# A second level of the seven-product scheme, over four batches at a time, in a graph network's aggregation

## The chip, the cores and the metric

The kernel runs on one core of one Trainium2 chip. All times are microseconds of device time of that core. Each is the median of the runs of one kernel, and every ratio is against runs of the kernel before on the same chip in the same rounds. Experiments sent at different times fell on two chips, on which the kernel before took 2066.7 and 2067.3, so differences between experiments of one or two us mean nothing. All runs told here were in the fast state.

## The reference, cut to what matters

Sixteen batches of 1024 nodes with 128 features pass through one plain graph layer (layer 0) and a gated layer of five steps (the GRU). Every step multiplies the same 1024 x 1024 adjacency matrix with the state of every batch; this product is called the aggregation.

```python
# layer 0
x = layernorm(x + (einsum('nm,bmo->bno', adj, x @ weight) + bias))
# layer 1, five times; in_matrix and out_matrix are both adj
m_in  = einsum('nm,bmd->bnd', in_matrix, h)
m_out = einsum('nm,bmd->bnd', out_matrix, h)          # the same product
av = concatenate([m_in, m_out], -1)
u3 = h @ u3_w.T + u3_b
z  = sigmoid(av @ w3_w.T + w3_b + u3)
r  = sigmoid(av @ w4_w.T + w4_b + u3)                 # u3 is common to z and r
hv = tanh(av @ w5_w.T + w5_b + (r * h @ u5_w.T + u5_b))
h  = (1 - z) * h + z * hv
# after the steps
x = layernorm(x + h)
```

All is fp32. There are six aggregations of sixteen batches (one in layer 0, five in the GRU).

## The kernel before

It already uses the seven-product scheme (seven block products in place of eight, paid for with sums of blocks) on one level. The adjacency is cut into 2 x 2 blocks, and a pair of batches makes the two block columns of the other factor. Each of the seven products is four matmuls of 512 columns (each of them two instructions in the trace). DVE (the vector engine) makes the four operand sums and adds the products up; the last batches' update lies under the next pair's first product.

```python
def sums(q, s):                      # operand sums of a pair: DVE, in SBUF
    nc.vector.tensor_sub(t[:, 0], block(q, 0, 1), block(q, 0, 0))
    nc.vector.tensor_sub(t[:, 1], block(q, 1, 1), t[:, 0])
    nc.vector.tensor_sub(t[:, 2], block(q, 1, 1), block(q, 0, 1))
    nc.vector.tensor_sub(t[:, 3], block(q, 1, 0), t[:, 1])

def product(n, pm, start):           # 4 matmuls, 512 columns each
    for c in range(CH):
        nc.tensor.matmul(pm, right[n][:, c, :], left[n][:, c, :],
                         start=(start and c == 0), stop=(c == CH - 1))

# [...] in aggregate: the chain of seven products and the adds out of PSUM
pa = bank("a"); product(1, pa, True);  nc.scalar.copy(p1, pa)
pb = bank("b"); product(6, pb, True);  nc.vector.tensor_add(u2, pb, p1)
product(2, pa, False);                 nc.scalar.copy(out_of[0, 0], pa)
product(7, pb, False);                 nc.vector.tensor_add(u3, pb, p1)
pc = bank("c"); product(5, pc, True);  nc.vector.tensor_add(out_of[1, 1], pc, u3)
product(4, pb, False);                 nc.vector.tensor_add(out_of[1, 0], pb, p1)
product(3, pc, False);                 nc.vector.tensor_add(out_of[0, 1], pc, u2)

# [...] in gates: u3 is copied to SBUF, and DVE adds it to both gates
nc.scalar.copy(u3[h], pu)
for w_t, b_t, dst in ((w4_t, br, rh_t[b]), (w3_t, bz, z_t[b])):   # [...] for each half of the columns
    nc.tensor.matmul(pg, w_t, m_t[b][:, cols], start=True, stop=True)
    nc.vector.tensor_add(dst[:, cols], pg, u3[h])
    nc.scalar.activation(dst[:, cols], dst[:, cols], AF.Sigmoid, bias=b_t)
```

The sixteen batches go in four groups of two pairs, each group through layer 0 and then its five steps.

## Time and profile before

| | before |
|---|---|
| median of the first three runs, lowest to highest | 2067.68, 2064.82 to 2069.21 us |
| profiled span, mean granted TensorE clock | 2062.0 us, 0.991 |
| TensorE (PE) busy | 96% |
| DVE / ScalarE (ACT) / GpSimd (POOL) busy | 53% / 27% / 7% |
| one GRU step of a pair, all of it TensorE busy | 43.19 us, so 86.4 us for four batches |

The page's first lines tell how long each engine was busy, the next ones the same in 40 slices of the span, in tenths; "PEclk" there is the share of its clock that TensorE was granted. The chain is what ended last, followed back from wait to wait. A line of a timeline has its start, its duration, the engine, the source line, the operation with what it writes and reads, the shapes, and how many instructions were taken together; at its end, in brackets, stands how long the engine had been idle and what it waited for. The lines that carry the reading are in the prediction below. They say that TensorE's own instruction stream is the time, and that DVE and POOL have room.

### The profile page before, as it was taken

How to read it: one execution, taken by the hardware profiler on the slowest of the kernel's cores; microseconds unless marked ns; L12 is line 12 of the kernel's file. 1: busy time of each engine (PE TensorE's matmuls, PEld its weight loads, DVE VectorE, ACT ScalarE, POOL GpSimd, SP SyncE). 2: the span in 40 equal slices, each digit the busy share in tenths (PEclk: the TensorE clock that was granted, in tenths of full speed). 3: DMA queues.
4: the chain of work that ended last, by engine and by line, in shares of the span. 5: the costliest groups of instructions: out<-in, count | busy, mean ns of one | idle time of the engine just before them, and what ended most of it. 6: DMA issues, size and time to landing. Idle time of an engine off the chain costs nothing.

```text
span 2062.0 us, 14771 instructions
## 1 busy us (share of the span) xinstructions
PE 1988.8 (96%) x5381; PEld 929.3 (45%) x5381; DVE 1100.5 (53%) x2284; ACT 563.0 (27%) x906; POOL 147.8 (7%) x190
## 2 busy tenths in 40 slices
PE   6999999999999999999989999999998999999994
PEld 4544444444444444444444444444444444444442
DVE  4544555446764554445675454455566544555447
ACT  1022333223103332233202322233220222333221
POOL 4200000001220000000231000000022000000001
PEclk9999999999999999999999999999999999999997
DMA  4000000000000000000000000000000000000000
GB/s 135 0 1 0 0 0 0 21 0 21 21 21 0 0 0 1 0 21 21 0 31 10 1 0 0 1 21 0 21 21 21 0 0 0 0 1 0 0 0 41
DMA packets 7561, 22.57 MB, mean 11 GB/s; under 512 B 1472, under 2 KB 2368, under 8 KB 7488
## 3 DMA queue, kind: packets, MB, share of 16 engines
q1 hardware_dynamic: 3168, 10.62, 1.5%
q0 software_dynamic: 2304, 8.39, 1.0%
q10 hardware_dynamic: 2016, 2.62, 0.4%
q8 instruction: 42, 0.69, 0.1%
q14 instruction: 31, 0.25, 0.0%
HBM read 13.24 MB, written 8.39 MB: 10 GB/s over the span
## 4 chain that ended last, share of the span: by engine, by line
PE 87%; DVE 9%; POOL 2%; DMA 1%; issue 1%; ACT 0%; POOLq 0%; ACTq 0%; SPq 0%; DVEq 0%
PE pb L199 20%; PE pc L199 13%; PE pg L275 13%; PE pa L199 13%; PE pu L268 6%; PE ph L287 6%; PE ph L286 6%; PE pt L307 3%; POOL rstd L162 2%; DVE stats L158 2%; DVE y L164 1%; DVE res L164 1%; DVE y L309 1%; DVE mv L159 1%; PE po L242 1%
## 5 line engine op out<-in xcount | busy, mean ns | idle before, releaser
L275 PE MATMUL pg<-m,w_t 128*128 128x512 f32 x640 | 291.9, 599 | 0.2
L270 ACT COPY u<-pu 128x512 f32<-128x512 f32 x160 | 92.2, 577 | 572.7 <-PE pu L268 572.7
L199 PE MATMUL pa<-a,rows 128*128 128x512 f32 x512 | 230.2, 592 | 0.0
L199 PE MATMUL pb<-a,t 128*128 128x512 f32 x512 | 230.2, 592 | 0.0
L275 PEld LDWEIGHTS pg<-m,w_t 128*128 128x128 f32 x640 | 118.3, 190 | 162.4 <-issue 124.4
L276 DVE TENSOR_TENSOR rh<-pg,u 128x512 f32<-128x512 f32 x160 | 110.7, 692 | 144.8 <-PE pg L275 144.8
L236 POOL TENSOR_TENSOR x<-x,b_bc 128x128 f32<-128x128 f32 x128 | 70.9, 566 | 1362.0 <-ACT hv L289 381.7
L286 PE MATMUL ph<-m,w_t 128*128 128x512 f32 x320 | 163.5, 592 | 0.0
L287 PE MATMUL ph<-rh,u_t 128*128 128x512 f32 x320 | 163.4, 592 | 0.0
L289 ACT ACTIVATE hv<-ph,bh 128x512 f32<-128x512 f32 x160 | 110.0, 687 | 176.2 <-PE ph L287 130.1
L290 DVE TENSOR_TENSOR hv<-hv,h 128x512 f32<-128x512 f32 x160 | 111.0, 694 | 83.4 <-ACT hv L289 83.4
L199 PEld LDWEIGHTS pb<-a,t 128*128 128x128 f32 x512 | 97.3, 190 | 122.5 <-issue 122.5
L268 PE MATMUL pu<-h,u_t 128*128 128x512 f32 x320 | 150.5, 592 | 0.0
L220 DVE TENSOR_TENSOR u3s<-pb,p 128x512 f32<-128x512 f32 x40 | 27.6, 691 | 217.9 <-PE pb L199 217.9
L199 PEld LDWEIGHTS pa<-a,rows 128*128 128x128 f32 x512 | 94.8, 190 | 107.1 <-issue 107.1
L277 ACT ACTIVATE rh<-rh,br 128x512 f32<-128x512 f32 x160 | 115.4, 722 | 85.7 <-DVE rh L276 80.5
L277 ACT ACTIVATE z<-z,bz 128x512 f32<-128x512 f32 x160 | 115.9, 724 | 41.5 <-DVE z L276 41.3
L199 PE MATMUL pc<-s,rows 128*128 128x512 f32 x256 | 115.1, 592 | 0.0
L199 PE MATMUL pc<-s,t 128*128 128x512 f32 x256 | 115.1, 592 | 0.0
L199 PE MATMUL pb<-s,t 128*128 128x512 f32 x256 | 115.1, 592 | 0.0
L291 DVE TENSOR_TENSOR hv<-hv,z 128x512 f32<-128x512 f32 x160 | 111.3, 696 | 3.7
L292 DVE TENSOR_TENSOR h<-h,hv 128x512 f32<-128x512 f32 x160 | 111.1, 694 | 3.9
(344 smaller groups left out, 2144.5 us busy)
## 6 DMA issues: line engine op xcount, KB each, us to landing
x<-in_x_dram SPq DMA_DIRECT2D x16, 512.0 KB, 4.4
out_dram<-y POOLq DMA_DIRECT2D x16, 512.0 KB, 3.0
adj<-in_adj_dram SPq DMA_DIRECT2D x4, 512.0 KB, 4.2
adj<-in_adj_dram ACTq DMA_DIRECT2D x4, 512.0 KB, 5.3
w_rows<-in_L_gnn_w_w_dram ACTq DMA_DIRECT2D x3, 128.0 KB, 3.9
u_rows<-in_L_gnn_u_w_dram ACTq DMA_DIRECT2D x2, 64.0 KB, 1.8
w_sb<-in_L_gnn_weight_dram SPq DMA_DIRECT2D x1, 64.0 KB, 6.9
b_bc<-in_L_gnn_bias_dram SPq DMA_DIRECT2D x1, 64.0 KB, 6.6
```

The costliest lines, as they stand in the source:

```text
L199: nc.tensor.matmul(pm, right[n][:, c, :], left[n][:, c, :], start=(start and c == 0), stop=(c == CH - 1), skip_group_check=True,)
L268: nc.tensor.matmul(pu, u3_t, h_t[b][:, cols], start=True, stop=True)
L270: nc.scalar.copy(u3[h], pu)
L275: nc.tensor.matmul(pg, w_t, m_t[b][:, cols], start=True, stop=True)
L276: nc.vector.tensor_add(dst[:, cols], pg, u3[h])
L277: nc.scalar.activation(dst[:, cols], dst[:, cols], AF.Sigmoid, bias=b_t)
L286: nc.tensor.matmul(pg, w5_t, m_t[b][:, cols], start=True, stop=False)
L287: nc.tensor.matmul(pg, u5_t, rh_t[b][:, cols], start=False, stop=True)
L289: nc.scalar.activation(hv, pg, AF.Tanh, bias=bh)
L290: nc.vector.tensor_sub(hv, hv, h_t[b][:, cols])
L291: nc.vector.tensor_mul(hv, hv, z_t[b][:, cols])
L292: nc.vector.tensor_add(h_t[b][:, cols], h_t[b][:, cols], hv)
```

## The change

The intent is to cut that stream. The scheme is applied twice: each of the seven block products over 512 x 512 blocks becomes seven products over 256 x 256 blocks, so 49 products stand for 64 where 56 stood. So that a block column of the inner level is still a whole batch of 128 features, four batches (a "quad") are taken together, and two outer products share one chain of seven inner ones: (1, 2) in the first chain, (3) alone in the single chain, then (6, 7) and (5, 4). Two further changes come with it. Layer 0 is done for all batches before the GRU, its result going to DRAM and back. And u3, the common term of the gates, is copied from PSUM into a second PSUM bank, so that both gates' matmuls add onto it and DVE's adds disappear (e1, which keeps this, returns the correct result).

```diff
+    def inner_sums(xs, dst, eng):                       # four sums
+        eng.tensor_sub(dst[0], xs(0, 1), xs(0, 0))
+        eng.tensor_sub(dst[1], xs(1, 1), dst[0])
+        eng.tensor_sub(dst[2], xs(1, 1), xs(0, 1))
+        eng.tensor_sub(dst[3], xs(1, 0), dst[1])
[...]
+    def outer_sums(src):                                # four sums of 1024 columns
+        nc.vector.tensor_sub(tsum[:, 0], hi[:, :, :CH], lo[:, :, :CH])
[...]
     def product(a, pm, start):
-        for c in range(CH):
-            nc.tensor.matmul(pm, right[n][:, c, :], left[n][:, c, :], ...)
+        for o, n in enumerate(ns):
+            for c in range(2):
+                nc.tensor.matmul(pm[:, ts(o, QT)], right[a][:, o, c, :], left[n][a][:, c, :], ...)
+        for hook in hooks.get(a, ()):
+            hook()                  # work of the batches before, between two products
[...]
+    def aggregate(tag, src, hooks):
+        chain(f"12_{tag}", src, (1, 2), into(first), hooks)
+        sums_of(src, (6, 7), nc.vector)
+        nc.vector.tensor_add(c11, two(first[:, 0]), two(first[:, 1]))
+        chain(f"3_{tag}", src, (3,), ..., hooks.get("late", {}))
+        sums_of(src, (5, 4), nc.gpsimd)
+        chain(f"67_{tag}", src, (6, 7), into(room[:, 0:2]), {})
+        nc.vector.tensor_add(p6, p6, first[:, 0])
+        nc.vector.tensor_add(p7, p7, p6)
+        nc.vector.tensor_add(c12, c12, two(p6))
+        chain(f"54_{tag}", src, (5, 4), into(room[:, 2:4]), {})
+        nc.vector.tensor_add(c21, two(p7), two(p4))
+        nc.vector.tensor_add(c22, two(p7), two(p5))
+        nc.vector.tensor_add(c12, c12, two(p5))
[...]  layernorm: the normalising itself moves from DVE to ScalarE
-            nc.vector.tensor_scalar(dst[:, c, :], y[:, c, :], mv[:, c, 0:1], rstd[:, c:c+1], ...)
+            nc.scalar.activation(y[:, c, :], y[:, c, :], AF.Identity, bias=shift[...], scale=rstd[...])
[...]  gates
-            nc.scalar.copy(u3[h], pu)
+            nc.scalar.copy(pz, pu)                       # PSUM to PSUM
+            nc.tensor.matmul(pu, w_t["w4"], agg[:, k, cols], start=False, stop=True, ...)
+            nc.scalar.activation(rh[:, cols], pu, AF.Sigmoid, bias=br)
+            nc.tensor.matmul(pz, w_t["w3"], agg[:, k, cols], start=False, stop=True, ...)
+            nc.scalar.activation(z[:, cols], pz, AF.Sigmoid, bias=bz)
-                nc.vector.tensor_add(dst[:, cols], pg, u3[h])
[...]  layer 0 of quad q, with the projections of quad q-1 between the products of its first chain
+        hooks = {6: [projection(0)], 2: [projection(1)], 7: [projection(2)], 5: [projection(3)]}
+        aggregate(f"x{q}", room, hooks)
[...]  a GRU step
+                def rest(tag=tag):
+                    back_to_rows(tag, 3)
+                    sums_of(rows, (3,), nc.gpsimd)
+                    outer_sums(rows)
+                hooks = {6: [lambda: back_to_rows(tag, 2)], 5: [rest]}
+            aggregate(tag, rows, hooks)
[...]
+            if not last:
+                sums_of(rows, (1, 2), nc.gpsimd)
+            update(tag, 3)
```

In the traces of the changed kernel L260 is the matmul of a product; L222 to L225 are the four inner sums and L243 to L246 the four outer ones; L281, L285, L288, L290 and L292 are the adds of a chain in order; L310 is the first combining add (c11), which stands once in each aggregation and marks the steps; L397 to L399 are the update of the hidden state; L206 and L207 are the statistics of the layer normalisation.

Two passages are cut out of the prediction, where it is marked: what they told of the hardware was not read from a trace or a run of this case. No term of its sum is cut: 91 + 3 x 58 + 8 + 20 x 85.4 + 26 + 22 is the 2029 that stands there, and the 0.215 us of a 256-column instruction is an estimate from the measured 0.429 (512 columns) and 0.11 (128). The lines after the first cut are POOL's and DVE's in the kernel before, while they prepare the adjacency's operands. That a POOL sum "delays DVE by its whole length" is the author's estimate from these lines, in which DVE's add takes 1.56 us for 0.69, so 0.87 more; 0.42 (DVE) and 0.73 (POOL) for 256 columns are estimates too, and the changed kernel's trace has 0.43 and 0.73 for them. That the clock granted to TensorE drops when DVE is late is shown by no line that the prediction quotes; in the changed kernel it was 0.50 after a wait of 4.92 us for a DVE add (below).

> **What bounds the kernel now.** I read the page's busy line and slices first, then the chain of work that ended last, then the groups of instructions with shapes kept apart, then stretches of the timeline.
>
> ```profile
> PE 1988.8 (96%) x5381; PEld 929.3 (45%) x5381; DVE 1100.5 (53%) x2284; ACT 563.0 (27%) x906; POOL 147.8 (7%) x190
> ...
> PE   6999999999999999999989999999998999999994
> ...
> PE 87%; DVE 9%; POOL 2%; DMA 1%; issue 1%; ACT 0%; POOLq 0%; ACTq 0%; SPq 0%; DVEq 0%
> ```
>
> TensorE is busy from end to end and carries 87% of the chain: the time is its instruction stream. Weight loads (PEld) run beside it; DVE has half the span free, POOL nearly all. The timeline of TensorE in one aggregation and in one projection gives the unit costs:
>
> ```profile
> 1002.19 3.60 PE L199 MATMUL pb<-a,t 128*128 128x512 f32 x8
> 1005.62 3.60 PE L199 MATMUL pc<-s,rows 128*128 128x512 f32 x8
> ...
> 55.94 1.95 PE L242 MATMUL po<-w_sb,m_-1_275 128*128 128x128 f32 x16
> 57.72 1.95 PE L242 MATMUL po<-w_sb,m_-1_276 128*128 128x128 f32 x16
> ```
>
> Each fp32 matmul of the program is two instructions. Eight with 512 columns start 3.43 us before the next eight: 0.429 us each, 0.84 ns a column. Sixteen with 128 columns take 1.78 us, 0.11 us each. So the price goes with the columns, and halving the columns must not cost a weight-load penalty: a 256-column instruction should take 0.215 us (an estimate). One GRU step of a pair is 43.19 us (the same gate group stands at 1670.51 and 1713.70 in the chain) and TensorE is busy for all 43.19 of them in the busy times of that stretch. The four groups repeat every 500.3 us (the first layer-0 projection of each group starts at 554.0, 1054.3, 1554.3), so a group is 10 x 43.19 = 432 plus 68 for its two layer-0 pairs.
>
> [...]
>
> ```profile
> 32.16 0.45 POOL L236 TENSOR_TENSOR x<-x,b_bc 128x128 f32<-128x128 f32 x1
> 32.57 1.72 POOL L104 TENSOR_TENSOR s<-a,s 128x512 f32<-128x512 f32 x1
> ...
> 36.80 1.27 POOL L104 TENSOR_TENSOR s<-a,s 128x512 f32<-128x512 f32 x1
> ...
> 32.48 0.69 DVE L102 TENSOR_TENSOR s<-a,a 128x512 f32<-128x512 f32 x1 [0.37 <-ACT a L99]
> 33.09 0.28 DVE L138 COPY w_t<-pt_w 128x128 f32<-128x128 f32 x1
> 33.29 1.56 DVE L103 TENSOR_TENSOR s<-s,a 128x512 f32<-128x512 f32 x1
> ```
>
> Alone a 512-column POOL add takes 1.27 us and a DVE one 0.69. The POOL add at 32.57 first waited for DVE's (1.72), then DVE's at 33.29 stood until POOL's was over (1.56). The two engines take turns, a whole instruction at a time. [...]
>
> **The change part by part.** Counts are per GRU step of four batches ("quad step"), of which there are 20, against 40 pair steps; a quad step of before is 2 x 43.19 = 86.4 us.
>
> *Removed on TensorE.* Aggregation was 2 x 28 matmuls of 512 columns, 112 instructions x 0.429 = 48.0 us. It becomes 49 x 2 matmuls of 256 columns, 196 x 0.215 = 42.2 us: 5.8 us less, an eighth. Gates stay at 80 x 0.429 = 34.3, transposes at 32 x 0.107 = 3.4. TensorE's floor: 79.9 us. Over 20 steps and 4 layer-0 quads the removal is 24 x 5.8 = 139 us, which would be the whole gain if nothing waited.
>
> *DVE.* Removed: the gate adds (L276), 16 x 0.69 = 11 us. Added: chains add 15 x 0.69 + 5 x 0.42 = 12.5 where 20 x 0.69 = 13.8 stood; seven combining adds of 1024 columns at an estimated 1.2 us (0.69 at 512 and 0.34 at 128 give 0.91 ns a column), 8.5; outer operand sums 4 x 1.2 = 4.9 and inner ones 4 x 0.69 = 2.8, for 8 x 0.69 = 5.5 before. Update and reset multiply remain 22.2. Sum 51 us of 80, against 53 of 86: not a bound by itself.
>
> *POOL*, idle in the steps before, gets eight sums of 512 columns (1.27) and four of 256 (about 0.73): 13 us. DVE's operations with two SBUF inputs are 38 us of its 51. By the turn-taking above each POOL sum that meets them delays DVE by its whole length.
>
> *ACT.* The common-term copy goes PSUM to PSUM instead of PSUM to SBUF, same number. Some 31 us a quad step: free.
>
> *What comes onto the path.* A product of the doubled scheme lasts 1.72 us (chain of two) or 0.86 (chain of one), where it lasted 3.43, and DVE's add must be done before the second product after it starts. I walked one steady step by hand in the engines' listed order with the durations above, t = 0 at the last gate matmul. (a) POOL's first sums start at -2.1, between DVE's updates, take turns with them, and the second operand is there at 3.7; TensorE wants it at 1.72: wait 2. (b) DVE, delayed so, ends its updates at 8.4; the first chain add is done at 9.1, TensorE waited since 8.1: 1. (c) The last batch's rows come at 14.4; now DVE has 4.9 of outer sums, POOL the single chain's sums, in turns; POOL's operand is there at 19.9, wanted at 17.8: 2. (d) That chain's first add stands behind inner sums and a combining add until about 26.5: 1. (e) The combining adds behind chain 67: 0.3. (f) Gates: bank rotation and copies, 0.5. Sum about 7 us; the step would be 87, nothing gained. Turn-taking at every meeting is the harshest reading; with half of it the waits are about 4. I take 5.5: 85.4 us a step.
>
> *Layer 0.* Per quad TensorE has 42.2 + 64 x 0.107 = 49. DVE has 31 of sums plus four projections of about 3.9 (two adds, eight statistics at 0.26 a piece, the small ones) = 47, and POOL's bias adds, sums and powers (29 us) hold it up a little. Normalising moves to ACT. I put a quad at 58 where before had 68 a group. The trip through DRAM (16 x 0.5 MB each way) is off the path: the loads of before took 4.4 us each and are issued long ahead.
>
> *Sum.* First layer-0 aggregation done at about 91 us (before had its second pair projected at 92; more operand preparation, no projection yet); 3 x 58 = 174; last projection partly exposed 8; 20 x 85.4 = 1708; first step of each group has transposes of the hidden state and unfinished normalising, 4 x 6.5 = 26; tail 22. Total 2029.
>
> **The rivals.** *TensorE stays the bound*: the waits vanish into its queue. For it: DVE is under two thirds busy; the schedule hoists other products over the waits. Against it: products are half as long and the order is fixed. It would give 2029 - 20 x 4.5 - 4 x 5 = about 1920. *The sums become the bound*: POOL and DVE in full turn-taking plus latencies that I left out, 88 to 90 us a step: 2080 to 2120. For it: walk (a) to (d). *Layer 0 through DRAM stalls the start*: x is loaded twice and saved rows come back; at 4.4 us a transfer against 49 us quads it should hide; if not, 10 to 30 us more. *Seeding costs*: the w4 matmul waits for the ACT copy of the same bank (0.58 us); in the listed order another matmul stands between, so below 0.5 us a batch.
>
> **Range and chances.** Waits of 2 to 9 us a step span 20 x 7 = 140 us, and layer 0 some 30 more; eight in ten lie in 1950 to 2095. Two per cent below 2067.7 is 2026, very near my centre, and waits must be about 5 or less for it. I give 0.46 to faster, 0.46 to the same, and 0.08 to slower, for which waits above 9 are needed. I predict 2028 us.
>
> **What would show it right or wrong.** In the profile after: 256-column instructions at 0.215 us apart (at 0.25 or more the saving is gone and my unit price is wrong). The quad step near 85 us with TensorE busy for about 80. Idle before TensorE put down to POOL and DVE sums (L222, L223, L243 to L246), at the second product of the first and single chains. POOL sums of 512 columns at 1.3 alone and up to 2 beside DVE; DVE's 1024-column sums up to 2.5 in these stretches. No DMA among the large releasers. What would make me wrong: contention smaller than the few early meetings suggest (then near 1920 to 1980), or DVE falling behind for whole stretches, so that the clock granted to TensorE drops as well (then above 2095).

## The result, and the profile after

| | before | after |
|---|---|---|
| median of four runs, lowest to highest | 2068.14, 2064.82 to 2069.21 | 2099.10, 2096.83 to 2100.06 |
| profiled span, clock | 2062.0, 0.991 | 2098.3, 0.976 |
| four batches' GRU step | 86.4 | 86.8 |

The ratio is 1.015, with a 95% interval of 1.013 to 1.017: slower by 1.5%. (Ratios here are the mean time of one kernel's fast runs over that of the other's of the same rounds, so not quite the ratio of the medians quoted.) That is inside the 2% that I called the same, but 70 us above the predicted time and just above the range. An eighth of the aggregation's TensorE work went, and no time with it.

The page's busy line, two rows of its slices and its chain, of the changed kernel:

```profile
PE 1913.4 (91%) x7401; PEld 1311.2 (62%) x7401; DVE 1385.9 (66%) x2191; ACT 710.6 (34%) x1258; POOL 511.9 (24%) x435
...
PE   5987888999999989999999999999999899999995
...
PEclk7999999999999999999999999999999999999997
...
PE 55%; DVE 23%; issue 3%; ACT 2%; POOL 2%; POOLq 0%; DVEq 0%; ACTq 0%
```

TensorE's busy time fell by 75 us (1988.8 to 1913.4), but its share of the chain fell from 87% to 55%, and DVE's rose from 9% to 23%. The bound has become a hand-over between TensorE and DVE. DVE is busy 285 us more than before, although its instructions got fewer (2284 to 2191) and by my sum the step had lost DVE work. That sum was wrong: it put 20 adds of products into four batches' step of before, and the code above has five a pair, so ten. The trace of before has 21.4 us of DVE in a pair's step, so 42.8, where I had 53. Without POOL's sums the changed step has 49.1 (e2 below), and with them 56.0: DVE's own work grew by 6 us a step, and POOL stretched it by 7. The slices 3 to 7, which are layer 0, are the weakest.

Two stretches of the busy times (start:end, length, then busy time and instructions of PE, PEld, DVE, ACT, POOL, then clock and DMA), one quad of layer 0 from one L310 to the next, and one steady step:

```profile
130.01:195.97 65.96, 54.69 (x263) 45.68 (x262) 47.55 (x120) 16.58 (x41) 28.52 (x44) 0.95 0.28 95
...
452.60:539.40 86.80, 82.50 (x310) 54.83 (x309) 56.01 (x67) 29.40 (x48) 18.75 (x12) 1.00 0.00 0
```

My sum had 51 us of DVE and 13 of POOL work in a step; the trace has 56.0 and 18.8. Each has 5 to 6 us more than I had counted, at full clock and with no DMA. In layer 0 a quad takes 66 us, not 58, with TensorE at a mean clock of 0.95 and idle for 11 us.

Now the place where a step begins. The timeline of TensorE, changed kernel:

```profile
400.84 1.89 PE L260 MATMUL pa<-a,rows 128*128 128x256 f32 x8
402.96 1.99 PE L260 MATMUL pb<-e,inner 128*128 128x256 f32 x8 [0.23 <-POOL inner L223]
...
405.66 1.89 PE L260 MATMUL pa<-a,rows 128*128 128x256 f32 x8
408.68 1.99 PE L260 MATMUL pb<-e,inner 128*128 128x256 f32 x8 [1.13 <-DVE first L281]
...
413.12 1.89 PE L260 MATMUL pb<-a,inner 128*128 128x256 f32 x8
414.84 1.89 PE L260 MATMUL pc<-e,rows 128*128 128x256 f32 x8
416.57 1.03 PE L260 MATMUL pa<-s,rows 128*128 128x256 f32 x4
418.80 1.10 PE L260 MATMUL pb<-e,inner 128*128 128x256 f32 x4 [1.21 <-DVE first L290]
...
424.08 0.70 PE L260 MATMUL pa<-s,tsum 128*128 128x256 f32 x2
426.46 1.13 PE L260 MATMUL pb<-s,inner 128*128 128x256 f32 x4 [1.69 <-DVE agg L281]
```

The two lines at 413.12 and 414.84 are 1.72 us apart, eight instructions each: 0.215 us, the price that I had taken. At full speed the instructions before a wait last 1.72 (eight), 0.86 (four) or 0.43 (two), so the second product of a chain could have begun at 402.56, 407.38, 417.43 and 424.51. It began 0.4, 1.3, 1.4 and 1.95 us later: 5.0 us a step. The four places are the (a), (b), (c) and (d) of my walk.

Whom they wait for shows in the timeline of DVE in the same stretch, changed kernel:

```profile
397.68 0.68 DVE L397 TENSOR_TENSOR hvs<-hvs,hid 128x512 f32<-128x512 f32 x1
398.40 1.70 DVE L398 TENSOR_TENSOR hvs<-hvs,tsum 128x512 f32<-128x512 f32 x1
400.20 1.57 DVE L399 TENSOR_TENSOR hid<-hid,hvs 128x512 f32<-128x512 f32 x1
401.70 1.75 DVE L397 TENSOR_TENSOR hvs<-hvs,hid 128x512 f32<-128x512 f32 x1
403.49 1.64 DVE L398 TENSOR_TENSOR hvs<-hvs,tsum 128x512 f32<-128x512 f32 x1
405.21 0.69 DVE L399 TENSOR_TENSOR hid<-hid,hvs 128x512 f32<-128x512 f32 x1
...
417.98 0.68 DVE L290 TENSOR_TENSOR first<-pb,first 128x512 f32<-128x512 f32 x1
...
422.12 2.29 DVE L310 TENSOR_TENSOR agg<-first 128x1024 f32<-128x1024 f32 x1
```

And that of POOL:

```profile
398.29 1.26 POOL L222 TENSOR_TENSOR inner<-rows 128x512 f32<-128x512 f32 x1 [57.98 <-ACT rows L411]
399.51 1.71 POOL L224 TENSOR_TENSOR inner<-rows 128x512 f32<-128x512 f32 x1
401.19 1.71 POOL L223 TENSOR_TENSOR inner<-rows,inner 128x512 f32<-128x512 f32 x1
402.98 1.59 POOL L225 TENSOR_TENSOR inner<-rows,inner 128x512 f32<-128x512 f32 x1
```

The update's three operations take 0.69 us each until POOL's first sum starts at 398.29. From then on, as long as POOL has sums in these lines, each DVE operation, all with two SBUF inputs, takes 1.57 to 1.75 us, and each POOL sum after the first 1.59 to 1.71: they alternate, one whole instruction of the one, then one of the other. When POOL is done (404.57) DVE is back at 0.69. L290 at 417.98, which has one input in PSUM, takes its 0.68 us while a POOL sum is running (L223, 416.94 to 418.64). L310, 1.22 us alone, takes 2.29, and it takes 2.28 or 2.29 in 16 of the 20 steps, all but the first of each group. At the third place (418.80) two sums end together: DVE's L290 at 418.66, which the profile names, and POOL's own L223 at 418.64, so POOL's lateness alone would have made that wait as long.

In layer 0 the same line of adds is late for another reason. TensorE's timeline in the third quad has one line for it:

```profile
184.57 3.78 PE L260 MATMUL pb_x<-a,inner 128*128 128x256 f32 x8 [4.92 <-DVE first L285]
```

and DVE's has what stood ahead of L285 in its queue:

```profile
181.89 0.41 DVE L212 SCALAR_TENSOR_TENSOR shift<-mv,rstd 128x8 f32<-128x8 f32 x1 [2.46 <-POOL rstd L210]
...
183.60 0.26 DVE L206 BATCH_NORM_STATS2 stats<-hid 128x6 f32<-128x128 f32 x1
183.86 0.65 DVE L285 TENSOR_TENSOR first<-pb_x,first 128x512 f32<-128x512 f32 x1
```

The projections of the quad before are hooked in between the products of the first chain, and each brings its normalisation with it. DVE waits 2.46 us for POOL's power, then goes through a batch's statistics, and only then makes the add that TensorE waits for. After those 4.92 us of idling the eight instructions take 3.78 us; 1.89 is normal. The clock granted from 184.5 to 188.4 is 0.50. So this wait costs twice, once as idle time and once as slow products. Shorter waits in layer 0 were followed by slow matmuls too: after 2.48 and 2.68 us (at 111.91 and 309.69) eight instructions of 128 columns took 2.08 and 2.07 us, where 1.05 is normal, at a granted clock of 0.50; after waits of 2.05 us they took 1.16 once and 1.45 once.

### The profile page after: what moved, and what is told of

Read it like the earlier page. It is cut to its first block, busy times and chain, and to the rows that moved or that the text cites. A ratio compares the mean times of both kernels' runs of the same rounds, so it can differ in the third digit from the quotient of the medians.

```text
span 2098.3 us, 20190 instructions
## 1 busy us (share of the span) xinstructions
PE 1913.4 (91%) x7401; PEld 1311.2 (62%) x7401; DVE 1385.9 (66%) x2191; ACT 710.6 (34%) x1258; POOL 511.9 (24%) x435
## 4 chain that ended last, share of the span: by engine, by line
PE 55%; DVE 23%; issue 3%; ACT 2%; POOL 2%; POOLq 0%; DVEq 0%; ACTq 0%
PE pb L260 14%; PE pc L260 9%; PE pu L377 7%; PE seeded L382 6%; PE pu L373 6%; PE pa L260 5%; DVE hvs L398 4%; PE ph L393 4%; PE ph L394 4%; DVE hvs L397 3%; DVE hid L399 3%; POOL rstd L210 2%; DVE tsum L244 1%; DVE inner L225 1%; DVE tsum L245 1%
## 5 line engine op out<-in xcount | busy, mean ns | idle before, releaser
L222 POOL TENSOR_TENSOR inner<-rows 128x256 f32<-128x256 f32 (+1 forms) x38 | 47.4, 1248 | 1077.8 <-ACT rows L411 1021.6
L260 PE MATMUL pb<-e,inner 128*128 128x256 f32 x720 | 179.3, 389 | 48.1 <-DVE first L281 25.1
L397 DVE TENSOR_TENSOR hvs<-hvs,hid 128x512 f32<-128x512 f32 x160 | 127.6, 799 | 90.7 <-ACT hvs L396 90.6
L260 PEld LDWEIGHTS pb<-e,inner 128*128 128x128 f32 x720 | 133.4, 191 | 85.5 <-POOL inner L223 35.4
L377 PE MATMUL pu<-agg,w_t 128*128 128x512 f32 x320 | 169.6, 612 | 0.0
L393 PE MATMUL ph<-agg,w_t 128*128 128x512 f32 x320 | 166.1, 601 | 1.1 <-ACT hvs L396 1.1
L394 PE MATMUL ph<-tsum,u_t 128*128 128x512 f32 x320 | 164.3, 595 | 0.0
L382 PE MATMUL seeded<-agg,w_t 128*128 128x512 f32 x320 | 163.4, 592 | 0.0
L373 PE MATMUL pu<-hid,u_t 128*128 128x512 f32 x320 | 157.1, 600 | 0.6 <-DVE ypad L424 0.6
L260 PE MATMUL pb<-s,inner 128*128 128x256 f32 x480 | 128.4, 390 | 27.8 <-DVE agg L281 26.9
L398 DVE TENSOR_TENSOR hvs<-hvs,tsum 128x512 f32<-128x512 f32 x160 | 141.3, 885 | 4.8
L260 PE MATMUL pc<-e,inner 128*128 128x256 f32 x560 | 137.8, 381 | 0.9 <-DVE first L292 0.9
L399 DVE TENSOR_TENSOR hid<-hid,hvs 128x512 f32<-128x512 f32 x160 | 123.6, 777 | 13.3 <-PE ph L393 0.5
L260 PEld LDWEIGHTS pb<-s,inner 128*128 128x128 f32 x480 | 85.2, 189 | 61.3 <-DVE agg L281 34.7
L260 PE MATMUL pb<-a,inner 128*128 128x256 f32 x480 | 120.7, 381 | 0.0
L260 PEld LDWEIGHTS pc<-e,inner 128*128 128x128 f32 x560 | 106.2, 191 | 17.2 <-DVE first L292 2.4
```

Of the source, the lines that this page charges most:

```text
L260: nc.tensor.matmul(pm[:, ts(o, QT)], right[a][:, o, c, :], left[n][a][:, c, :], start=(start and o == 0 and c == 0), stop=(c == 1), skip_g ...
L373: nc.tensor.matmul(pu, w_t["u3"], hid[:, k, cols], start=True, stop=True, skip_group_check=True)
L377: nc.tensor.matmul(pu, w_t["w4"], agg[:, k, cols], start=False, stop=True, skip_group_check=True)
L382: nc.tensor.matmul(pz, w_t["w3"], agg[:, k, cols], start=False, stop=True, skip_group_check=True)
L393: nc.tensor.matmul(ph, w_t["w5"], agg[:, k, cols], start=True, stop=False)
L394: nc.tensor.matmul(ph, w_t["u5"], rh[:, cols], start=False, stop=True)
```

## The experiments

My theory after this reading: (A) POOL's sums and DVE's operations with two SBUF inputs take turns, DVE's queue runs late by that, and the products wait; (C) in layer 0 the statistics in DVE's queue do the same. The main rival to A is (B): DVE simply has too much to do at the start of a step, or POOL's results come too late because POOL is slow, in which case it is no matter of turns.

**e1_sums_on_dve: the same sums on the busier engine.** All of POOL's operand sums in the GRU steps go to DVE, in the same places. Under A this helps, under B it harms: DVE gets 12 sums a step more.

```diff
-        sums_of(src, (5, 4), nc.gpsimd)
+        sums_of(src, (5, 4), nc.gpsimd if tag[0] == 'x' else nc.vector)
[...]  both places that make the single chain's sums
-                    sums_of(rows, (3,), nc.gpsimd)
+                    sums_of(rows, (3,), nc.vector)
[...]
-                sums_of(rows, (1, 2), nc.gpsimd)
+                sums_of(rows, (1, 2), nc.vector)
```

> All sums of the GRU steps that POOL made are made by DVE, result correct. Theory A (the 6.8 us of waits in an 86.8 us step come mainly from POOL's sums: late, and holding DVE by turns[...]): DVE gains 7 us of work but loses its blocked time (operations of 0.69 us that took 1.6 to 1.75, a 1.23 us one that took 2.3), so the step falls to 83 to 85 us and the whole to about 2040 to 2065. Rival B (DVE's own first-in-first-out queue of 4.9 us of outer sums and 1.2 us combining adds sets the waits, whoever makes the small sums): the step stays at 86 to 89 us, the whole at 2095 to 2140.

Measured: 2012.3 us, ratio 0.974 (0.972 to 0.975), correct. That is 87 us under the changed kernel, more than A expected. A steady step is 81.4 us. The busy line of its page, and then two lines of its DVE timeline, a sum that has moved and the combining add:

```profile
PE 1893.2 (94%) x7401; PEld 1314.6 (65%) x7401; DVE 1369.0 (68%) x2415; ACT 705.9 (35%) x1258; POOL 175.2 (9%) x211
```

```profile
398.22 0.68 DVE L224 TENSOR_TENSOR inner<-rows 128x512 f32<-128x512 f32 x1
...
417.89 1.22 DVE L310 TENSOR_TENSOR agg<-first 128x1024 f32<-128x1024 f32 x1
```

DVE has 224 instructions more than in the changed kernel and is busy 17 us less. The sums cost it no more than they had cost it while POOL did them. In four steady steps (361 to 680 us of the span) the waits show TensorE idle for nobody. B is refuted.

**e2_no_pool_sums: the same sums nowhere.** They are left out, so the result is wrong on purpose (relative error 0.32). It bounds what any other placement could give.

```diff
-        sums_of(src, (5, 4), nc.gpsimd)
+        if tag[0] == 'x':
+            sums_of(src, (5, 4), nc.gpsimd)
[...]  and the three other calls with nc.gpsimd in the GRU steps removed
```

> The sums of the GRU steps that POOL makes are left out (stale operands, wrong result on purpose). Theory A: waits (a) and (c) and the blocked DVE time vanish, the step falls to 81.5 to 83 us, the whole to about 1985 to 2025. Rival B: DVE's queue alone keeps most of the waits, the step stays above 84.5 us and the whole above 2050.

Measured: 2016.8 us, ratio 0.976, steps of 81.7 us. It is no faster than e1 on the same chip. So once POOL is out of the way TensorE sets the step, and DVE's extra work is hidden. The 81.4 us of e1, with TensorE busy for all of them, are 1.5 above the 79.9 us of my count of instructions; that much is left when no product waits for a sum, and it was not taken apart.

**e6_idle_pool_sums: the contention alone.** From e1, in 16 of the 20 steps POOL repeats the sums (1, 2), (3) and (5, 4), at the same times, into a place that nobody reads. Nothing waits for POOL, so if its lateness were the matter (A2) the time would stay at e1's; if it is the taking of turns (A1) it comes back.

```diff
+    def idle_sums(src, ns):
+        dst = [...]                      # parts of ypad, which is free then
+        inner_sums(blocks_of(src, ns), dst, nc.gpsimd)
[...]
+        if tag[0] != 'x' and tag[-1] != '0':
+            idle_sums(src, (5, 4))
[...]
                     sums_of(rows, (3,), nc.vector)
+                    idle_sums(rows, (3,))
[...]
                 sums_of(rows, (1, 2), nc.vector)
+                idle_sums(rows, (1, 2))
```

> DVE makes the real sums of the GRU steps as in the first experiment (steps of 81.4 us), and in 16 of the 20 steps POOL makes the same sums again into a place that TensorE does not read; nothing in the step waits for their result. Theory A1 (turn-taking[...] is the cost): DVE's operations with two SBUF inputs are stretched again, the steps rise by 3 us or more, the whole from 2012 to 2045 or above. Theory A2 (only the lateness of POOL's results cost anything): steps stay at 81.4 to 82 us, the whole at 2010 to 2022.

Measured: 2175.0 us, ratio 1.052, correct: 163 us more than e1, for results that no one uses; 10 us in each of the 16 steps, whose period is now about 91. Its DVE timeline (its lines are shifted: L318 is the combining add) and its POOL timeline:

```profile
420.40 1.75 DVE L224 TENSOR_TENSOR inner<-tsum 128x512 f32<-128x512 f32 x1
422.07 1.75 DVE L223 TENSOR_TENSOR inner<-tsum,inner 128x512 f32<-128x512 f32 x1
423.75 2.28 DVE L318 TENSOR_TENSOR agg<-first 128x1024 f32<-128x1024 f32 x1
```

```profile
419.89 1.71 POOL L224 TENSOR_TENSOR ypad<-tsum 128x512 f32<-128x512 f32 x1
421.56 1.71 POOL L223 TENSOR_TENSOR ypad<-tsum,ypad 128x512 f32<-128x512 f32 x1
```

And what TensorE waited for from 330 to 720 us (microseconds in total, times, longest), where e1 has nothing:

```profile
PE pb L268 <- DVE inner L223: 10.1, 4, 2.7
PE pb L268 <- DVE first L298: 8.3, 4, 2.1
PE pu L387 <- DVE agg L318: 7.5, 4, 3.1
```

Only DVE's operations are waited for, none of POOL's. The delay comes through the taking of turns alone: A1 is shown, A2 refuted as the whole. In the changed kernel itself the first and shortest of the four waits was for a POOL sum, and at the third a POOL sum ended at the same time as DVE's add, so there lateness has some share.

**e11_first_sums_dve: which of the waits.** From the changed kernel, only the sums of the first chain (1, 2) go to DVE. They are what meets the updates, steps (a) and (b) of the walk.

```diff
             if not last:
-                sums_of(rows, (1, 2), nc.gpsimd)
+                sums_of(rows, (1, 2), nc.vector)
```

> Of the changed kernel's POOL sums only those for the first chain (four of 512 columns a step, in 16 steps) go to DVE; the other two sets stay on POOL. The prediction's walk put about 3 of the 7 us of waits a step on these (its points a and b). If that split is right, the step falls from 86.8 to 83.5 to 84.3 us, the whole by 40 to 53 us to 2046 to 2059. If the sets of the single chain and of the last chain cost nearly all (points c and d), the step stays above 85.5 us and the whole above 2078.

Measured: 2067.6 us, ratio 1.000 (0.998 to 1.002): 31.5 us under the changed kernel, 2.0 us in each of the 16 steps that have such sums. The walk had 3 us for (a) and (b), so this missed both expectations, lying between them. The trace of the changed kernel has 1.7 us for them (0.4 and 1.3), which fits. The waits of this run from 330 to 720 us are exactly the other two, unchanged:

```profile
PE pb L260 <- DVE agg L281: 6.9, 4, 1.7
PE pb L260 <- DVE first L290: 4.8, 4, 1.2
```

So the waits can be taken away one by one, and they add up: 2.0 here, and 5.4 (86.8 to 81.4) with all sums moved.

**e4_one_level: what the second level is worth.** The inner level is undone: the seven outer products are plain matmuls of 512 columns again, in the new order of quads, with no inner sums.

```diff
+        def direct(name, ns, dest, hooks):
+            for o, n in enumerate(ns):
+                for k in range(2):
+                    for c in range(CH):
+                        nc.tensor.matmul(pm, right[n][:, k, c, :], outer[n][:, c, :], ...)
+                    nc.scalar.copy(dest(o, k), pm)
[...]
-        chain(f"12_{tag}", src, (1, 2), into(first), hooks)
+        direct(f"12_{tag}", (1, 2), flat_into(first), hooks)
[...]  the other chains alike; all sums_of(...) and inner_left(...) removed
```

> The second level is undone: each of the seven outer products is done directly with 512 columns (112 instructions of 0.429 us a quad step for 196 of 0.215), everything else of the change stays (four batches, layer 0 first through DRAM, seeded gates); result correct. By the unit prices TensorE's floor rises by 5.8 us to 85.7 us a step, while POOL's sums, 15 + 5 chain adds and the inner sums on DVE vanish and 14 copies come on ACT. Theory A (the second level's saving is eaten by its own sums): the step is 86 to 87.5 us, the whole 2065 to 2110, level with the changed kernel. Rival (four batches or seeding cost the time, not the second level): the step comes out at 89 us or more, the whole above 2140. Rival (the one-level step also has long waits because outer sums remain): 88 to 90 us.

Measured: 2106.1 us, ratio 1.019, correct; steps of 86.7 us with TensorE 96% busy. The second level as built has the same step, 86.8: TensorE idles for what it saves. It also follows that the rest of the change (quads, layer 0 first, seeded gates, normalising on ScalarE, and here 14 copies of products a step on ScalarE for 8) costs some 39 us against before, of which 20 x 0.3 = 6 are in the steps; in which parts the rest arises was not taken apart.

**e8_no_seed: the seeded PSUM banks.** From e1, the gates add u3 on DVE again, with five rotating banks in place of three and two seeded ones.

```diff
-            nc.scalar.copy(pz, pu)
+            nc.scalar.copy(u3, pu)                      # to SBUF
-            ... pu, w_t["w4"], agg[:, k, cols], start=False, stop=True, ...
-            nc.scalar.activation(rh[:, cols], pu, AF.Sigmoid, bias=br)
+            nc.tensor.matmul(pr, w_t["w4"], agg[:, k, cols], start=True, stop=True)
+            nc.vector.tensor_add(rh[:, cols], pr, u3)
+            nc.scalar.activation(rh[:, cols], rh[:, cols], AF.Sigmoid, bias=br)
[...]  pz alike
```

> On top of the first experiment the third part of the change is undone: the gates' common term is copied to SBUF and DVE adds it to both gates, as the kernel before did, with five rotating banks for three. DVE gets 16 more operations of 0.69 us a quad step (11 us), so about 69 of 81 us busy. If seeding is needed to keep DVE from becoming the bound, the step rises from 81.4 to 83 to 87 us, the whole to 2045 to 2125. If DVE had room for it, the step stays below 82 us and the whole below 2025.

Measured: 2026.1 us, ratio 0.980, correct; steps of 82.3 us, DVE 77% busy. That is 14 us more than e1 and between the two expectations: seeding is worth about 1 us a step once POOL is silent, although DVE has room on average. It does not explain the missing gain.

**e3_late_norm: the statistics out of the first chain.** In layer 0 only the projections stay in the first chain; bias, statistics and normalising of each batch are hooked into the third and fourth.

```diff
-        layernorm(y, f"0_{b}")
-        nc.sync.dma_start(saved_rows(b), y)
+        def normalise():
+            [...]                       # bias, layernorm and store as before
+        return normalise
[...]
+            hooks["67"] = {1: [norm], 5: [norm]}
+            hooks["54"] = {1: [norm], 5: [norm]}
```

> In layer 0 the bias adds, statistics and normalising of the four batches of the quad before are put into the third and fourth chain of a quad instead of between the adds of its first chain; same work, result correct. Theory C (layer 0 takes 58 us a quad instead of 49 because the chain's adds stand behind about 14 us of statistics in DVE's queue, up to 4.9 us at a time, after which the first products also run at half clock): three quads fall from 58 to 51 to 54 us, the whole by 12 to 20 us to about 2080 to 2087, and the granted clock in layer 0 rises from about 0.94 to 0.98 or more. Rival D (layer 0 is bound by the sum of DVE's and POOL's work or by the loads through DRAM): the period stays at 57 or 58 and the whole within 5 us of 2099.

Measured: 2080.7 us, ratio 1.007 (1.005 to 1.008), 18 us under the changed kernel, as C expected for the whole. By the starts of L310 the three quads take 51.6, 60.2 and 56.5 us where they took 63.9, 66.0 and 66.0; C had 51 to 54 for each, so only the first got there. Of these 27 us, 8 are given back in the passage to the GRU. The steps stay at 86.8. The edit moves POOL's bias adds, DVE's statistics and ScalarE's normalising together; their shares were not separated. The busy times of two quads show the clock (the last-but-two column) at full:

```profile
65.42:117.06 51.64, 49.17 (x253) 42.09 (x251) 41.86 (x68) 3.30 (x6) 21.83 (x40) 1.00 0.13 42
117.06:177.27 60.21, 51.47 (x261) 43.80 (x260) 48.28 (x121) 16.69 (x40) 30.86 (x45) 1.00 0.31 105
```

**e5_dve_late_norm: both together** (the edit of e1 on top of that of e3).

> Both changes at once: sums of the GRU steps on DVE (2012.3 alone) and layer 0's normalising in later chains (18.4 us less alone). If the two causes lie in different stretches and add up, as theories A and C say, the whole is 2012.3 - 18.4 = 1994, within 5 us. If both only removed the same kind of wait somewhere else, it is above 2003.

Measured: 1993.1 us, ratio 0.964 (0.963 to 0.966). From e1 the late normalising takes 19 us, from the changed kernel it took 18: the two causes add up, and 106 us of the changed kernel's time are accounted for.

**e9_best: the same for the last normalising.** From e5, in the first step of a group the normalising of the finished batches 2 and 3 of the group before is moved from the first to the third and fourth chains.

```diff
-        layernorm(y, f"1_{b}")
-        nc.sync.dma_start(as_rows(b, out), y)
+        def normalise():
+            layernorm(y, f"1_{b}")
+            nc.sync.dma_start(as_rows(b, out), y)
+        return normalise
[...]
-                    hooks = {6: [lambda: finish(q - 1, 2)], 5: [lambda: finish(q - 1, 3)]}
+                    ends = []
+                    hooks = {
+                        6: [lambda: ends.append(finish(q - 1, 2))],
+                        5: [lambda: ends.append(finish(q - 1, 3))],
+                        "67": {1: [lambda: ends.pop(0)()]}, "54": {1: [lambda: ends.pop(0)()]},
+                    }
[...]  the other calls of finish run what it returns at once
```

> As the combination of both changes, and the last normalising of batches 2 and 3 of a group is also put into the later chains of the next group's first step. In the changed kernel that first step took 92.8 us for 86.8, the wait of 1 to 1.5 us at each transpose and add behind statistics. Theory C says 3 to 6 us less per group change, three of them: 10 to 18 us below the combination, about 1976 to 1986. If the statistics of that step are not the cause, it is level with the combination.

Measured: 1984.1 us, ratio 0.960 (0.958 to 0.961), correct. This is 9 us less than e5, a little under the expected gain. By the starts of L310 each of the three changes of groups got 2.3 us shorter, 7 in all; the profiled runs differ by another 4.6 us before the first GRU step, where nothing was edited. It beats both kernels: 4.0% under the one before and 5.5% under the changed one.

**e10_layer0_dve: the layer-0 sums too.** From e9, POOL's operand sums in layer 0 go to DVE as well.

```diff
-        sums_of(src, (5, 4), nc.gpsimd if tag[0] == 'x' else nc.vector)
+        sums_of(src, (5, 4), nc.vector)
[...]
-        sums_of(room, (3,), nc.gpsimd)
+        sums_of(room, (3,), nc.vector)
```

> On top of the best version so far (1984.1) the sums that POOL still makes in layer 0 go to DVE too (eight of 512 or 256 columns a quad, four quads). POOL keeps the bias adds, so turn-taking is not gone. If the sums cost there what they cost in the steps (about 5 us a time), the whole falls by 10 to 20 us to 1964 to 1974. If DVE, with 47 us of 58 busy in layer 0, is full there, the whole stays within 5 us or rises.

Measured: 1997.5 us, ratio 0.966, correct: 13 us more than e9, where I expected 10 to 20 us less if the taking of turns were the cost there as well. It went the way that I had given to the rival, a DVE with no room there, but the traces do not bear that out simply: from 66 to 293 us DVE is busy for 175 us here and for 177 in e9. By the starts of L310 the kernel is 6 us late in the first quad already (70.1 for 64.4) and 11 at the first GRU step (322.5 for 311.7). Half of the loss thus lies in the start, where DVE also makes the adjacency's operands; which operation is late after that was not isolated and stays open. "Take it from POOL" is no rule for every place.

## Why the prediction was wrong, point by point

- **The unit price was right.** A 256-column instruction takes 0.215 us. TensorE's work in a step is what I counted, within 1.5 us (81.4 in e1 against 79.9).
- **The mechanism was named, and the walk was right as a sum.** I walked a step by hand with turn-taking at each meeting and got 87 us; it is 86.8. Piece by piece (a) was 0.4 for 2, (b) 1.3 for 1, (c) 1.4 for 2, (d) 1.95 for 1, and 1.5 us of the rest, for which I had 0.8 under (e) and (f), stay in e1. The pieces were not right each; that their errors cancelled so nearly is in part luck.
- **The step that failed** is the one after it: "Turn-taking at every meeting is the harshest reading; with half of it the waits are about 4. I take 5.5: 85.4 us a step." Nothing that I quoted from the profile of before spoke for the discount. The timelines of e6 and of the changed kernel show turn-taking at every meeting in the stretches printed, and the stretched L310 in 16 of 20 steps. It is no worst case but how it went. 20 x (86.77 - 85.4) is 27 us, and it alone would have carried 2028 to 2055: the walk's own answer was "nothing gained".
- **DVE's work in the step of before was misread**, as said above: 53 us for 42.8, from 20 adds where ten stood. So the change gave DVE more work and not less. It was not the step that failed, since e1 has no waits with that work and more on DVE, but it made the change look lighter for DVE than it was.
- **Layer 0 was mis-sized.** I had a quad at 58 us; the three took 63.9, 66.0 and 66.0, together 22 more than my 174. I had counted DVE's 47 us there, but not that they stand ahead of the adds in one queue, nor that the idle time is followed by products at half the clock (1.89 becomes 3.78). e3 took out 18 us of it.
- **Smaller terms.** With layer 0's last products done at 291 us instead of 91 + 174 = 265, the start has some 4 us besides the quads. The passage into the GRU is about 7 longer than the 14.5 that I gave it (its first L310 comes 40.8 us after its first product, 21.3 in a steady step, and that product starts 2 us after layer 0's last). The changes of groups are as I had them: 19.0 us together, for 19.5. The tail is 31 for 22 (the last L310 is at 2001.67 and the span ends at 2098.3; 65 of these 97 us are the rest of a step). 27 + 22 + 4 + 7 + 9 = 69, where 70 are to be explained. The tail I read only and did not test.
- **The rivals.** "The sums become the bound", with 2080 to 2120, is what came, though by a step of 86.8 and layer 0 and not by 88 to 90 a step. "TensorE stays the bound" (1920) would have needed more than a silent POOL: with none of its sums in the steps e2 is at 2017, and even e9 is at 1984. "Layer 0 through DRAM stalls" did not happen: apart from the adjacency's own load at the start (6.9 us in two waits) no DMA is among TensorE's larger waits; a load of x or of saved rows takes 3.3 to 4.9 us. "Seeding costs" was wrong in its sign, taken as a whole: it is worth about 1 us a step (e8, with POOL silent).
- **Where the 139 us went.** 20 x 5.8 = 116 of them lie in the steps, where the count of instructions fell from 85.7 to 79.9 us. They came back as 6.9 us a step of waits and gaps (79.9 to 86.8), of which 5.4 were caused by POOL's sums. The other 23 lie in layer 0, where idling and half clock took more than that.

## What to carry to other kernels

An idle engine is not free help. Before work is given to it, look for operations of the two that take turns: here a DVE operation with two SBUF inputs that took turns with POOL's sums of 512 columns took 0.9 to 1.1 us longer (1.57 to 1.75 for 0.69, 2.29 for 1.22), more than the 0.68 us in which DVE makes such a sum itself, so the same sum on the busier engine was cheaper, and sums that no one read cost 163 us. When a hand walk with measured durations gives an unwelcome answer, keep it, and discount it only by something that a trace shows. And put work that nobody is waiting for (statistics, normalising) where no urgent add stands behind it in the same engine's order: that move gave 18 us here and cost nothing.
